# Two attention blocks in one kernel: layer 1's norm folded into weights, exponent and quotient, and the next sample's Q/K moved ahead of the projection

## The chip, the cores and the metric

The kernel runs on one core of one Trainium2 chip. The core has TensorE (matrix products, PE in the profile, with its weight loads shown apart as PEld), VectorE (DVE), ScalarE (ACT), GpSimd (POOL) and SyncE (SP), which issues nearly all DMAs. The metric is the device time of one execution in microseconds; lower is better. Before the change it is 2942.72 us, the median of three runs (2942.66 to 2943.72). The profiled execution took 2943.53 us, of which 2941.7 us lie between its first and its last instruction; all places in time below count from that first instruction.

## What is computed

For each of eight samples, an array of 512 channels by 1024 positions in f32, two attention layers run one after the other:

```python
def layer0(x):                      # 8 heads of 64 channels
    h = group_norm(x, 32 groups) * norm_w + norm_b
    q, k, v = split(qkv_w @ h + qkv_b)
    o = per head: softmax(q k^T / 8) v
    return x + proj_w @ o + proj_b

def layer1(x):                      # one head of 512 channels
    n = (x - mean) * rsqrt(var + eps)     # over the whole sample
    n = n * gn_gamma + gn_beta
    q, k, v = wq @ n + bq, wk @ n + bk, wv @ n + bv
    o = softmax(q k^T / sqrt(512)) v
    return x + wo @ o + bo
```

## The kernel before

**Joined weights.** Layer 1 never makes k, nor applies wo apart: before the loop `product` multiplies wq with wk and wv with wo into two weights, `wqk1` and `wvo1`. With them the scores are (wqk n)^T n, and the values are already projected. The biases go through the same products in `Through`: rows of bias copies times a weight, stored to DRAM, fetched back as columns and added up (`made["bias_q1"]`, `made["bias1"]`).

**Products in seven parts.** Every big product is a Strassen-Winograd step (`strassen`): seven half-size products of parts `A11` to `S4` of the one operand and `B11` to `T4` of the other. `finish` makes the `S` parts of a weight, `Combined` the `T` parts of the data. Partial results stay in one PSUM bank (`line`, copied by ScalarE to a tile `u`) and another (`single`). `strassen` is a generator that yields after each product; `together` takes two of them turn by turn, and `at_steps` hangs other work (hooks) on the numbers of these steps. TensorE, ScalarE and VectorE run in exactly the order in which the program was written (`manual_schedule`); SyncE's and GpSimd's orders are a scheduler's.

**One sample.** `layer0` makes v, then the second half of the heads' q and k (`pairs_qk(w, 1, ...)`), in whose steps the next sample's group norm is taken and its `T` parts are made. It then runs through 64 units (four pairs of heads in `ORDER`, two halves of the positions, eight blocks of keys): `scores` (L630), exp on ScalarE (L557), the running sum of the exponentials `acc` on VectorE (L559), and `values` two units later (L649). For a pair, `add_keys` (L663) multiplies `acc` with ones to add up over keys; `one_over` (L570) takes the reciprocal, `spread` (L579) copies it by DMA to the rows where it is wanted, `divide` (L669) applies it. The last pair, `end`, is treated half by half: the first half in the loop of units, the second in the first step of `project`, where VectorE's reciprocal stands ahead of the product's further parts (`combine1`, `combine2`, L713 and L719).

`project` (matmuls at L438) adds the result to x (L766) and takes the statistics of each finished piece at once (`of_half`, L297); `of_channels` (L300) ends them. After it the first half of the heads' q and k of the next sample is computed (`pairs_qk(..., 0, ...)`), and in its steps 4 to 9 the layer-1 norm is taken: the average of the means by a small matmul (`mean_of_all`, L278), the spread and its average (`variance_of_all`), the power -1/2 on GpSimd (L318), scale and shift applied to the data, x to `h` (`normed`, L336 and L338), and the `T` parts of `h`. For the last sample there is no next one, and these steps stand alone.

`attention1` then makes q from `h` (L438 again, bias added at L468 and L470), v (L453), the scores (L844), exp with a constant scale (L854), and the values (L901); at L929 and L930 the reciprocal and the bias are applied and x is added.

**Weights.** `next_weight` hands out a weight and asks for the one two places further on in the list `coming`; three buffers hold them. The first use of a weight loads four parts, finishes the `S` parts on VectorE and stores all seven to DRAM; later ones load the seven. Everything is issued on SP in one queue.

Of the kernel before, what the change touches and what calls it, by code (L numbers as in the profile page):

```python
# [58 lines left out]
def two_attention_blocks(  # L60
# [103 lines left out]
    extent = const.tile([P, B * 12], FP, tag="extent", name="extent")  # L164
# [16 lines left out]
    def finish(parts, a21):  # L181
        nc.vector.tensor_tensor(parts["S1"], a21, parts["A22"], ALU.add)
        nc.vector.tensor_tensor(parts["S2"], parts["S1"], parts["A11"], ALU.subtract)
        nc.vector.tensor_tensor(parts["S3"], parts["A11"], a21, ALU.subtract)
        nc.vector.tensor_tensor(parts["S4"], parts["A12"], parts["S2"], ALU.subtract)
# [4 lines left out]
    class Weight:  # L190
# [25 lines left out]
        def finish(self):  # L216
            for parts, rest in zip(self.parts, self.rest):
                finish(parts, rest)
            stored[self.name] = dram.tile([P, W_SIZE], FP, tag=self.name, name=f"stored_{self.name}")
            nc.sync.dma_start(stored[self.name], self.tile)  # L220
# [16 lines left out]
    for b in range(B):  # L237
        coming += ["qk13", "p0"] if b == 0 else ["v0", "qk13", "p0"]
        coming += ["qk02"] if b + 1 < B else []
        coming += ["wqk1", "wvo1"]  # L240
# [42 lines left out]
    class Norm:  # L283
# [3 lines left out]
        def __init__(self, xs, w, b, average, name):  # L287
            self.xs, self.w, self.b, self.average, self.name = xs, w, b, average, name
# [25 lines left out]
        def variance_of_all(self):  # L314
            var = self.average(self.spread, f"v_{self.name}")
            rstd = self.tile("rstd")
            nc.vector.tensor_scalar(rstd, var, EPS, None, ALU.add)
            nc.gpsimd.tensor_tensor(rstd, rstd, minus_half[:, : self.width], ALU.pow)  # L318
            scale = self.scale = self.tile("scale", NC)
            shift = self.shift = self.tile("shift", NC)  # L320
            w, b = vec[:, self.w : self.w + NC], vec[:, self.b : self.b + NC]
            if self.width == 1:
                nc.vector.tensor_scalar(scale, w, rstd, None, ALU.mult)
                nc.vector.tensor_scalar(shift, scale, self.mean, None, ALU.mult)
            else:
                nc.vector.tensor_tensor(scale, rstd, w, ALU.mult)
                nc.vector.tensor_tensor(shift, self.mean, scale, ALU.mult)
            nc.vector.tensor_tensor(shift, b, shift, ALU.subtract)

# [10 lines left out]
    def norm0(xs, b):  # L340
        return Norm(xs, V_NW0, V_NB0, group_average, f"0_{b}")

    def norm1(xs, b):
        return Norm(xs, V_NW1, V_NB1, sample_average, f"1_{b}")

    class Combined:
# [5 lines left out]
        def first(self, quarters):  # L352
            (b11, b12), (b21, b22) = quarters
# [3 lines left out]
            nc.vector.tensor_tensor(self.parts["T1"], b12, b11, ALU.subtract)  # L357
            nc.vector.tensor_tensor(self.parts["T2"], b22, self.parts["T1"], ALU.subtract)
            self.b12 = b12

        def second(self):
            p = self.parts
            nc.vector.tensor_tensor(p["T3"], p["B22"], self.b12, ALU.subtract)
            nc.vector.tensor_tensor(p["T4"], p["B21"], p["T2"], ALU.subtract)

    def combined(quarters, name):
        c = Combined(name)
        c.first(quarters)
        c.second()
        return c.parts  # L370
# [4 lines left out]
    def strassen(multiply, done, name):  # L375
# [11 lines left out]
        line = banks("s", f"ps_{name}_0")[:, 0, :]  # L387
        multiply(line, "A11", "B11", True)
        copied(1)
        single = banks("o", f"ps_{name}_1")  # L390
        single, spare[0] = single[:, 0, :], single[:, 1, :]
# [99 lines left out]
    def many(v_bias, name):  # L491

        t = tile2(f"many_{name}")[:, 0, :P].rearrange("p (c m) -> p c m", c=NC)
        at = vec[:, v_bias : v_bias + NC]
        nc.vector.tensor_copy(t, at.unsqueeze(2).to_broadcast([P, NC, P // NC]))
        return t

    class Through:
# [4 lines left out]
        def __init__(self, moving, many, bias, name, ps):  # L503
            self.bias, self.name, self.ps = bias, name, ps
            for cc in range(NC):
                for to, w in moving(cc):
                    rows = ps[cc * (P // NC) : (cc + 1) * (P // NC), to]
                    nc.tensor.matmul(rows, many[:, cc, :], w, start=True, stop=True)

        def store(self):  # L510
            row = tile2(f"row_{self.name}")[:, 0, :]
            nc.scalar.copy(row, self.ps)
            self.shares = dram.tile([NC, C], FP, tag=self.name, name=f"shares_{self.name}")
            for cc in range(NC):
                nc.sync.dma_start(self.shares[cc : cc + 1], row[cc * (P // NC) : cc * (P // NC) + 1, :])

        def fetch(self):
            self.columns = const.tile([P, NC, NC], FP, tag=f"c_{self.name}", name=f"c_{self.name}")
            for cc in range(NC):
                nc.sync.dma_start(  # L520
                    self.columns[:, cc, :], self.shares[cc].rearrange("(o p) -> p o", p=P)
                )

        def add(self):
# [927 lines left out]
```

## Time and profile before

| | |
|---|---|
| median of three runs | 2942.72 us |
| span of the profiled execution | 2941.7 us |
| mean granted TensorE clock | 0.997 |
| instructions | 33922 |
| reciprocal of 128x512 on VectorE, mean | 3355 ns |
| 128x512 elementwise on VectorE with two tensors, mean | 680 to 692 ns |
| the same with a column and two tensors, mean | 733 to 752 ns |
| 128x1024 combination on VectorE, mean | 1217 to 1225 ns |
| period of a sample, start of one `project` reciprocal wait to the next | 359.91 us |

In a line of a timeline the first number is the start, the second the length, then follow the engine, the line of the kernel, the operation, output and inputs with their shape, and the number of instructions merged into the row; in brackets stands how long the engine was idle before it, and on whom it had waited. An f32 matmul is recorded as two instructions. The ends of matmuls are modelled, so two rows may overlap by a tenth or two of a microsecond; starts are measured.

### The profile page before, as it was taken

The numbers are of one execution on the slowest core, as the hardware profiler recorded it, in microseconds if no ns is written. First come the engines' busy times: TensorE is split into PE (matmuls) and PEld (weight loads), VectorE is DVE, ScalarE is ACT, GpSimd is POOL, SyncE is SP. The second block draws the span as 40 slices with busy tenths as digits, with TensorE's granted clock in tenths as the row PEclk, the third lists the DMA queues.
The fourth block names the chain that finished last, engine by engine and source line by source line (L and its number), as shares of the span: only waits on it lengthen the run. The fifth ranks groups of instructions, "written<-read, shape, count | busy, mean of one in ns | idle before, by whom it ended". The sixth has DMA issues, their size and how long they took to land.

```text
span 2941.7 us, 33922 instructions
## 1 busy us (share of the span) xinstructions
PE 2912.1 (99%) x14018; PEld 1357.8 (46%) x14018; DVE 1753.0 (60%) x2142; ACT 1069.8 (36%) x1512; POOL 13.9 (0%) x26
## 2 busy tenths in 40 slices
PE   9999999999999999999999999999999999999898
PEld 4434554345533455335553354533545335453353
DVE  4586265853668536684357844578355773547825
ACT  2462214622156221552216522264222642226321
POOL 0000000000000000000000000000000000000000
PEclk9999999999999999999999999999999999999999
DMA  7301122011220103102031021210212112120001
GB/s 269 133 23 51 50 93 79 23 50 50 93 87 16 68 33 118 62 16 75 25 118 62 15 76 54 89 64 23 80 47 96 56 33 75 43 96 20 8 0 37
DMA packets 63403, 184.27 MB, mean 63 GB/s; under 512 B 13309, under 2 KB 13821, under 8 KB 56841
## 3 DMA queue, kind: packets, MB, share of 16 engines
q1 hardware_dynamic: 63096, 182.01, 18.1%
q8 instruction: 112, 1.84, 0.3%
q14 instruction: 51, 0.41, 0.0%
q10 hardware_dynamic: 144, 0.02, 0.0%
HBM read 137.41 MB, written 27.81 MB: 56 GB/s over the span
## 4 chain that ended last, share of the span: by engine, by line
PE 95%; DVE 4%; ACT 1%; issue 0%; DMA 0%; SPq 0%; POOL 0%; DVEq 0%; POOLq 0%
PE s L630 15%; PE ps_o L649 14%; PE ps_v L453 13%; PE ps_o L901 13%; PE ps_q L438 13%; PE ps_s L844 13%; PE ps_k L438 7%; PE ps_p L438 4%; DVE inv L570 1%; PE ps_sum L663 1%; DVE acc L559 1%; PE ps_wvo L540 1%; PE ps_wqk L540 0%; DVE t_p L713 0%; DVE t_p L719 0%; ACT p L557 0%
## 5 line engine op out<-in xcount | busy, mean ns | idle before, releaser
L557 ACT ACTIVATE p<-s 128x1024 f32<-128x1024 f32 x512 | 523.5, 1024 | 313.6 <-PE s L630 310.9
L630 PE MATMUL s<-q,k 64*64 64x512 f32 x4096 | 532.5, 591 | 0.0
L649 PE MATMUL ps_o<-p,v 64*64 64x512 f32 x4096 | 528.7, 589 | 0.0
L559 DVE TENSOR_TENSOR acc<-acc,p 128x1024 f32<-128x1024 f32 x384 | 468.4, 1220 | 80.2 <-ACT p L557 62.9
L630 PEld LDWEIGHTS s<-q,k 64*64 64x64 f32 x4096 | 151.9, 133 | 294.7 <-issue 254.4
L649 PEld LDWEIGHTS ps_o<-p,v 64*64 64x64 f32 x4096 | 156.6, 133 | 282.8 <-issue 280.3
L852 DVE TENSOR_TENSOR p<-ps_s,u_s 128x512 f32<-128x512 f32 x96 | 66.4, 691 | 249.8 <-ACT u_s L385 139.4
L487 DVE TENSOR_TENSOR v<-ps_v,u_v 128x512 f32<-128x512 f32 x96 | 66.1, 689 | 202.3 <-PE ps_v L453 130.6
L385 ACT COPY u_v<-ps_v 128x512 f32<-128x512 f32 x96 | 56.2, 585 | 326.4 <-PE ps_v L453 326.4
L385 ACT COPY u_q<-ps_q 128x512 f32<-128x512 f32 x96 | 56.2, 585 | 317.4 <-PE ps_q L438 317.3
L844 PE MATMUL ps_s<-s_q,t 128*128 128x512 f32 x384 | 167.4, 592 | 0.0
L901 PE MATMUL ps_o<-t_p,s_v 128*128 128x512 f32 x384 | 166.1, 592 | 0.0
L559 DVE TENSOR_TENSOR acc<-p,p 128x1024 f32<-128x1024 f32 x64 | 78.4, 1224 | 98.9 <-ACT p L557 98.9
L438 PE MATMUL ps_p<-t_p,w_p 128*128 128x512 f32 x256 | 113.3, 595 | 5.4 <-DVE inv L570 5.4
L470 DVE SCALAR_TENSOR_TENSOR q<-ps_q,bias_q,u_q 128x512 f32<-128x512 f32 x48 | 36.0, 750 | 137.0 <-ACT u_q L385 74.8
L844 PEld LDWEIGHTS ps_s<-s_q,t 128*128 128x128 f32 x384 | 73.0, 190 | 91.8 <-issue 91.8
L901 PEld LDWEIGHTS ps_o<-t_p,s_v 128*128 128x128 f32 x384 | 73.0, 190 | 91.8 <-issue 89.9
L901 PE MATMUL ps_o<-p,v 128*128 128x512 f32 x256 | 113.3, 595 | 0.0
L453 PE MATMUL ps_v<-w_wvo,t 128*128 128x256 f32 x512 | 113.1, 379 | 0.0
L438 PE MATMUL ps_q<-t,w_wqk 128*128 128x512 f32 x256 | 112.5, 592 | 0.0
L844 PE MATMUL ps_s<-q,h 128*128 128x512 f32 x256 | 112.5, 592 | 0.0
L570 DVE RECIPROCAL inv<-ps_sum 128x512 f32<-128x512 f32 x32 | 107.4, 3355 | 7.1 <-ACT held_sum L566 7.1
(208 smaller groups left out, 3593.2 us busy)
## 6 DMA issues: line engine op xcount, KB each, us to landing
x<-in_x SPq DMA_DIRECT2D x92, 512.0 KB
w_qk<-stored_qk SPq DMA_DIRECT2D x14, 1792.0 KB
out<-x SPq DMA_DIRECT2D x32, 512.0 KB
w_wqk<-stored_wqk SPq DMA_DIRECT2D x8, 1792.0 KB
w_wvo<-stored_wvo SPq DMA_DIRECT2D x8, 1792.0 KB
w_v<-stored_v SPq DMA_DIRECT2D x7, 1792.0 KB
w_p<-stored_p SPq DMA_DIRECT2D x7, 1792.0 KB
inv<-inv SPq DMA_DIRECT2D x192, 64.0 KB
```

What stands on the lines that cost most here:

```text
L385: nc.scalar.copy(us[n], line)
L438: nc.tensor.matmul(bank, w[a][:, k, c * P : (c + 1) * P], bs[b][:, k, :], start=fresh and k == 0, stop=k == 1, skip_group_check=True,)
L453: nc.tensor.matmul(bank[:, u * 2 * P : (u + 1) * 2 * P], bs[b][:, k, n * P : (n + 1) * P], w[a][:, k, :], start=fresh and u == k == 0, sto ...
L487: nc.vector.tensor_tensor(v, pairs(bank), pairs(u), ALU.add)
L557: nc.scalar.activation(p, s, AF.Exp, scale=factor)
L559: nc.vector.tensor_tensor(acc, first, p, ALU.add)
L570: nc.vector.reciprocal(inv, ps)
L630: nc.tensor.matmul(s[cols, j, :], flat(ks[pair])[rows, k0 : k0 + HD], qs[pair][rows, g, :], start=True, stop=True,)
L649: nc.tensor.matmul(o[cols, half, :], vs[kt][rows, c0 : c0 + HD], p[rows, j, :], start=kt == 0, stop=kt == NT - 1,)
L844: nc.tensor.matmul(bank, bs[b][:, k, t * P : (t + 1) * P], q_parts[a][:, k, :], start=fresh and k == 0, stop=k == 1, skip_group_check=True,)
L852: nc.vector.tensor_tensor(p, bank, u, ALU.add)
L901: nc.tensor.matmul(bank, v_parts[kt // 2][a][:, kt % 2, c * P : (c + 1) * P], p_parts[kt // 2][b][:, kt % 2, :], start=fresh and kt == 0, ...
```

## The change

- **Layer 1 no longer norms the data.** Gamma is multiplied into the rows of `wvo1` and `wqk1` (`scale_rows`) and into q as ScalarE's scale; the constant part of the norm goes through the weights as further bias rows (`Rows` and `Through` with two sets of rows, for beta and for gamma); 1/deviation squared becomes part of exp's scale (`norm.factor`), and 1/deviation a factor of the quotient (`norm.rstd`). q, v and the scores are made of raw x. Mean and deviation are needed for q's bias (`untaken`: `norm.c`) and for the last bias (`bias`).
- **The two averages, the `T` parts of x and the small operations after them move into the steps of q's own product** in `attention1`. `strassen` gets the argument `fine`, which adds a step after the first product.
- **The next sample's first Q/K goes ahead of the projection**, right after the units. The last pair is then summed over both halves at once in its step 3, its reciprocal spread by DMA like the others', the division done at step 8 and the rest of the projection's parts at step 9. Only the last sample keeps the old order (`last`). The list `coming` is reordered to suit.
- **Scaling and finishing of `wvo1` and `wqk1` move to GpSimd**; the rows for `wvo1` go into the product of `wqk1`, those for `wqk1` into step 3 of the first Q/K.

```diff
-        coming += ["qk13", "p0"] if b == 0 else ["v0", "qk13", "p0"]
+        coming += ["qk13"] if b == 0 else ["v0", "qk13"]
         coming += ["qk02"] if b + 1 < B else []
-        coming += ["wqk1", "wvo1"]
+        coming += ["p0", "wqk1", "wvo1"]
...
+        def scale_rows(self, engine, by):
+            for cc in range(NC):
+                for _, a in self.moving(cc):
+                    engine.tensor_scalar(a, a, vec[:, by + cc : by + cc + 1], None, ALU.mult)
...
+        def untaken(self):
+            rstd, mean = self.rstd, self.mean
+            over, self.c, self.factor = self.tile("over"), self.tile("c", NC), self.tile("factor")
+            nc.vector.reciprocal(over, rstd)
+            nc.vector.tensor_scalar(self.c, made["q_g"], mean, None, ALU.mult)
+            nc.vector.scalar_tensor_tensor(self.c, made["q_b"], over, self.c, ALU.mult, ALU.subtract)
+            nc.vector.tensor_scalar(self.factor, rstd, rstd, C**-0.5, ALU.mult, ALU.mult)
...
+        if not last:
+            name = f"0_{b}_{end}"
+            hooks = {
+                1: [combine1],
+                2: [lambda: combine2(2, 0), lambda: combine2(3, 0), lambda: combine2(4, 0)],
+                3: [lambda: sum_both(end, room(f"sum_{name}"), name)],
+                6: [lambda: held(invs.pop(end), f"inv_{name}")],
+                8: [lambda: divide_both(end)],
+                9: [lambda: combine2(2, 1), lambda: combine2(3, 1), lambda: combine2(4, 1)],
+            }
+            at_steps(
+                together(*pairs_qk(next_weight(), 0, combine.parts, qs_next, ks_next, b + 1)), hooks
+            )
...
-                first = i == half == 0
+                first = last and i == half == 0
...
-        at_steps(together(*[
-            make_channels(
-                w, c, c, bs, made["bias_q1"], lambda chunk, half: piece(qs, chunk, half), f"q_1_{b}"
-            )
-            for c in range(2)
-        ]), {})
+        combine, later = Combined(f"1_{b}"), []
+        combine.take(xs)
+        bs = combine.parts
...
+            return strassen(by_channels(w, c, bs), done, f"q_1_{b}_{c}", True)
+        at_steps(together(make_q(0), make_q(1)), {
+            0: [norm.mean_of_all, lambda: combine.make(1)],
+            1: [norm.deviation],
+            2: [norm.untaken],
+            3: [lambda: combine.make(2), lambda: later.pop(0)(), lambda: later.pop(0)()],
+            5: [lambda: combine.make(3)],
+            7: [lambda: combine.make(4)],
+        })
+        bias = norm.bias()
...
-                nc.scalar.activation(p, bank, AF.Exp, scale=C**-0.5)
+                nc.scalar.activation(p, bank, AF.Exp, scale=norm.factor)
...
-                    nc.vector.tensor_tensor(u, bank, invs[1][:, j, :], ALU.mult)
                     nc.vector.scalar_tensor_tensor(
-                        x, u, made["bias1"][:, chunk : chunk + 1], x, ALU.add, ALU.add
+                        u, bank, norm.rstd, invs[1][:, j, :], ALU.mult, ALU.mult
+                    )
+                    nc.vector.scalar_tensor_tensor(
+                        x, u, bias[:, chunk : chunk + 1], x, ALU.add, ALU.add
                     )
...
-        wvo1.finish()
         spare[0] = banks("o", "ps_norm")[:, 0, :]
-        manys = [many(V_BV1, "bias1"), many(V_BQ1, "bias_q1")]
-        taken = product(wqk1, nq1, nk1, "s", [norm.mean_of_all, norm.variance_of_all])
+        norm1_vectors = many(V_NB1, "norm1", V_NW1)
...
+                super().__init__(sets, 2, name, ps)
+                self.store()
+                w.scale_rows(nc.gpsimd, V_NW1)
...
+            wvo1.finish(nc.gpsimd)
...
+        taken = product(wqk1, nq1, nk1, "s", {
+            (0, 3): [through_v], (2, 1): [norm.mean_of_all], (2, 3): [norm.variance_of_all]
+        })
...
-            together(*pairs_qk(w, 0, bs, qs, ks, 0)), {2: [wqk1.finish], 8: [waiting[0].finish]}
+            together(*pairs_qk(w, 0, combine.parts, qs, ks, 0)), {3: [through_q], 8: [waiting[0].finish]}
```

## The prediction

> **What bounds the kernel now.** I read the busy totals and the chain of waits first, then TensorE's own timeline for its gaps, then the other engines inside each gap.
>
> ```profile
> PE 2912.1 (99%) x14018; PEld 1357.8 (46%) x14018; DVE 1753.0 (60%) x2142; ACT 1069.8 (36%) x1512; POOL 13.9 (0%) x26
> PE 95%; DVE 4%; ACT 1%; issue 0%; DMA 0%; SPq 0%; POOL 0%; DVEq 0%; POOLq 0%
> ```
>
> TensorE is busy for 2912.1 of 2941.7 us. The work taken off VectorE and ScalarE (the layer-1 norm's passes over the data) is beside it and worth nothing by itself. Only what TensorE executes, or the 30 us in which it waits, can move the time. A 512-column record of its starts 0.429 us after the one before (eight take 3.43 us). In a middle sample its timeline has one wait, in the projection:
>
> ```profile
> 594.63 3.70 PE L438 MATMUL ps_p<-o,w_p 128*128 128x512 f32 x8
> 598.82 1.55 PE L438 MATMUL ps_p<-t_p,w_p 128*128 128x512 f32 x3 [0.50 <-DVE inv L570]
> ```
>
> 594.63 + 3.43 = 598.06, so 0.76 us are lost to the reciprocal of the last head pair. The timeline of all engines at the end of that projection:
>
> ```profile
> 614.38 1.88 PE L438 MATMUL ps_p<-o,w_p 128*128 128x512 f32 x4
> ...
> 616.09 3.60 PE L438 MATMUL ps_q<-x,w_qk 128*128 128x512 f32 x8
> ...
> 617.42 0.67 DVE L780 TENSOR_TENSOR u_p<-ps_p,u_p 128x512 f32<-128x512 f32 x1
> ...
> 618.13 0.75 DVE L766 SCALAR_TENSOR_TENSOR x<-u_p,bias,x 128x512 f32<-128x512 f32 x1
> ...
> 618.91 0.69 DVE L297 BATCH_NORM_STATS2 part<-x 128x6 f32<-128x512 f32 x1
> ...
> 619.52 0.47 DVE L300 BATCH_NORM_AGGREGATE stat<-part 128x2 f32<-128x12 f32 x4
> ```
>
> TensorE is through with the projection at 616.09 and goes straight on with the next Q/K; VectorE has the statistics of x only at 619.99, 3.9 us later. Now nobody waits for them. In the last sample there is no next Q/K, and TensorE's timeline shows the wait in the open:
>
> ```profile
> 2774.44 1.88 PE L438 MATMUL ps_p<-o,w_p 128*128 128x512 f32 x4
> 2780.11 0.59 PE L278 MATMUL ps_m<-stat,in_sample 128*128 128x4 f32 x2 [3.79 <-DVE stat L300]
> 2781.62 0.59 PE L278 MATMUL ps_v<-spread,in_sample 128*128 128x4 f32 x2 [0.92 <-DVE spread L312]
> 2784.65 5.64 PE L438 MATMUL ps_q<-h,w_wqk 128*128 128x512 f32 x8 [2.44 <-DVE h L338]
> ```
>
> The eight records after it take 5.64 us in place of 3.60. The view by stretches says why (columns: stretch, length, busy PE, PEld, DVE, ACT, POOL, granted clock, DMA):
>
> ```profile
> 2396.07:2399.49 3.42, 1.86 (x6) 0.55 (x4) 3.39 (x3) 1.63 (x3) 0.00 (x0) 1.00 0.00 0
> 2399.49:2402.90 3.41, 3.41 (x8) 1.56 (x9) 3.41 (x6) 0.00 (x0) 0.00 (x0) 1.00 0.00 0
> 2774.95:2778.36 3.41, 1.37 (x4) 0.30 (x2) 3.31 (x6) 0.00 (x0) 0.00 (x0) 1.00 0.01 2
> 2778.36:2788.60 10.24, 5.13 (x9) 2.86 (x10) 7.41 (x21) 3.06 (x5) 0.55 (x1) 0.50 0.00 0
> ```
>
> After 1.37 us of work in 3.41 the clock is halved; after 1.86 it is not.
>
> **What the Trainium skill says.** "TensorE: Matmul & The Clock Gate", Part 1 (The HAM clock gate), gives a free-running window of 3.413 us, after an idle one of which the clock is halved until a busy one. The trace agrees on the grid (10.24 us is three windows), not on "idle": 1.37 us of work did not save the clock. "GPSIMD Engine Reference", section 3.1, gives 4497 ns for a two-input f32 operation of 2048 elements on GpSimd, so I estimate 1.12 us for 512; the trace has no such operation there.
>
> **The change part by part.**
>
> *Gains on TensorE.* (1) The last pair's sums are taken once over both halves: two groups of 128*64 records (8.6 us over 8 samples each, 1.08 per group) become one of 128*32 (25.6/192 x 8 = 1.07), in seven samples: -7.5 us. (2) With the next Q/K (24 us) ahead of the projection, the reciprocal and the copies of its result are hidden: a copy like it took from 2371.8 to 2380.2, 8.4 us; the sum can be taken 11.4 us into the stage, ScalarE's read and the reciprocal end near 15.7, the copies near 24, and the projection reads the divided half near 27. So the new wait on DMA costs nothing by 3 us. The division's ten VectorE operations (3.35 + 1.22 + 8 x 0.68 = 10.0 us) and ScalarE's two come into a stage in which VectorE was busy for 13.2 of 24.6 us, and the old norm's leave it. Weight requests move too: the projection's weights are asked for after those of this Q/K, still a stage (24 us) ahead, against 6 us for such a transfer (50.96 to 56.97). The gaps removed are 0.76 in five samples, 1.13 in the first, 1.83 in the seventh: -6.8 us. (3) The last sample's norm: the projection ends at 2776.16, and the first eight Q records end at 2790.29 where 3.43 us would do: -10.3 us, allowing for the two averages. Gains: 24.6 us.
>
> *The wait that appears.* In every sample layer 1's Q now follows the projection at once. TensorE's order is: first product of one half (four records, 1.72 us), the average of the means, first product of the other half, the average of the spreads. The first needs raw x, which is there; the average needs the statistics, which come 3.95 us after the projection's end, as VectorE's tail (6 pieces, all in the same order) is unchanged. Queued behind that small matmul is everything TensorE has. 3.95 - 1.72 = 2.23, with refilling 2.3 us, eight times: +18.4 us. The second average is hidden: its input took 1.14 us (628.11 to 629.25), the product ahead of it 1.72. POOL's power (0.55 us), the four small operations after it and the extra scalings on ScalarE fit ahead of what needs them by a microsecond or more. T1 to T4 of raw x (1.22 us each) come a product ahead of their use. Exp with a scale from memory, the quotient's extra factor (0.75 for 0.69 us) and the bias lie beside TensorE.
>
> *Before the loop.* Two sets of bias rows, each 4 products of 512 and 8 of 256 columns in 32-column groups, cost 2.1 us each (the rows of before: 8 records in 0.88, 16 half as wide in 1.02, transitions 0.2); 1.95 us of old rows go. The first set delays the norm's averages by 2.1, so the start of Q (38.27) too. The scaling of W_vo and its combinations go to POOL ahead of the power:
>
> ```profile
> 32.70 1.01 POOL L318 TENSOR_TENSOR rstd<-rstd,minus_half 128x4 f32<-128x4 f32 x1 [30.70 <-DVE rstd L317]
> ...
> 38.27 3.70 PE L438 MATMUL ps_q<-x,w_qk 128*128 128x512 f32 x8 [0.73 <-ACT rest_wqk L550]
> ...
> 50.96 0.45 SPq L220 DMA_DIRECT2D stored_wqk<-w_wqk  x1
> ...
> 58.31 2.27 SPq L119 DMA_DIRECT2D x<-in_x  x4
> ```
>
> POOL starts near 26.9; eight scalings near 0.4 us (guessed between memset's 0.20 and affine select's 0.34 for half the width, doubled) and four combinations of 1.12 make 7.7, to 34.6; the power could start at 34.8. Taken: 0.5 us late, bounds 0 and 6. Q starts +2.6, and the second set adds 2.1: +4.7. The same POOL work on W_qk holds SP's queue: its store moves from 51 to about 61.5, and behind it stand the weights of the second Q/K, another store, a reload and the next x. At the rates of the stretches 52 to 56 (a store, 455 GB/s) and 60 to 68 us (x, 345 GB/s) these 6.6 MB take 16 us and x is complete near 86, while V, starting near 67.4, needs VectorE past two of its four parts at 86.2. Taken: +1.5, bounds 0 and 8.
>
> *The clock.* A 2.1 us idle stretch that falls wholly within one window leaves 1.3 us of work, like the window that halved the clock. Between 1.37 and 1.86 the limit is unknown, so 0.4 to 0.65 of all phases trip it. A tripped window costs 1.6 us. The phases aren't random: the period, 359.91 us less 1.9 plus 2.3, is 105 windows and 1.9; from a miss the next sample lands in a hit, and a hit's own 1.6 us brings the period to 106 windows less a trifle, which repeats the hit. Lowest: nothing; highest: all eight, 13 us. Taken: six, +9.5, and +1.5 for the stalls before the loop.
>
> Sum: 18.4 + 4.7 + 1.5 + 11.0 - 24.6 = +11.0: 2952.7 us against this profile's span of 2941.7, or 2953.7 beside the other runs (2942.7, a microsecond above the span).
>
> **Rivals.** *The clock holds.* Without the 11.0 the sum is 0: 2943 us, no change. For it: the window before 2399.49 held with 1.86. Against it: the new stretch is longer than that one. It decides if a window with 1.3 us of work doesn't trip. *Faster: the statistics come early.* Were VectorE not behind at the projection's end, its last piece needs 0.68 + 0.75 + 0.69 + 0.47, about 2.5 us; the wait is then 0.8, the clock holds, and 2931 us follow. It decides from a lead of 1.4 us. Against it: VectorE is busy without a break over the last six pieces, and none of that work is removed. *POOL is slow before the loop.* At twice the estimate Q starts 8 us later and x comes late by as much again: about 2968. For it: nothing in the trace bounds those operations from above. That Q/K ahead waits for the copies of the reciprocal is within the range.
>
> **How the numbers follow.** My forecast 0.52 (2946 to 2961), clock holds 0.22 (2939 to 2948), statistics early 0.11, slow POOL 0.15. Two in ten are left out by 2941 to 2966. A measurement tells 0.2%, 5.9 us, from no change: slower gets nearly all of the first and the fourth, 0.63; same 0.25; faster 0.12.
>
> **What would show it.** Right: in each sample an idle of about 2.1 us ahead of the average of the means, released by the statistics, and half clock after most; no gap on the reciprocal but in the last sample; Q of sample 0 near 41. Wrong: an idle under 1 us there, or a clock that stays whole.

## The result

The changed kernel takes 2969.34 us (median of four runs, 2968.41 to 2972.41), the kernel before 2943.09 (four runs, 2942.66 to 2943.72): a ratio of 1.0091, 95% interval 1.0073 to 1.0108. It is slower, as forecast, but by 26.2 us where 11.0 were forecast, and 3 us above the range. The profiled execution has a span of 2967.1 us at a mean granted clock of 0.993 (before: 2941.7 at 0.997).

TensorE's own timeline splits the difference. The first run of sixteen score products of layer 0 (`s<-q,k ... x16`) marks the end of all that is done once. In the kernel before, the products of V (`ps_v`) start at 62.41, the second Q/K follows at 86.58 and the score run at 115.90; in the changed kernel the score run starts at 138.42:

```profile
62.41 7.07 PE L453 MATMUL ps_v<-w_v,x 128*128 128x256 f32 x32
...
86.58 3.60 PE L438 MATMUL ps_q<-x,w_qk 128*128 128x512 f32 x8
...
115.90 1.95 PE L630 MATMUL s<-q,k 64*64 64x512 f32 x16
```

```profile
138.42 1.95 PE L681 MATMUL s<-q,k 64*64 64x512 f32 x16
```

| | start of the score run | from there to the end |
|---|---|---|
| before | 115.90 | 2825.8 |
| changed | 138.42 | 2828.7 |
| difference | +22.5 | +2.9 |
| by the prediction's terms | +7.7 | +3.3 |

The second column of the last row is 18.4 + 9.5 - 24.6, the first 4.7 + 1.5 + 1.5. So the loop as a whole did what was forecast, and nearly all that is missing lies ahead of it.

**The loop.** The busy totals and the chain of waits of the changed kernel:

```profile
PE 2917.9 (98%) x14050; PEld 1363.1 (46%) x14050; DVE 1720.0 (58%) x2135; ACT 1088.3 (37%) x1500; POOL 38.7 (1%) x52
PE 93%; DVE 4%; POOL 1%; DMA 1%; SPq 0%; ACT 0%; issue 0%; DVEq 0%; POOLq 0%; ACTq 0%
```

VectorE's 33 us less busy time bought nothing, as said. POOL's share of the chain, 0% before, is 1%. TensorE's timeline of a middle sample, from the projection on:

```profile
998.71 7.03 PE L477 MATMUL ps_p<-o,w_p 128*128 128x512 f32 x16
1005.57 12.18 PE L477 MATMUL ps_p<-t_p,w_p 128*128 128x512 f32 x28
...
1022.74 1.88 PE L477 MATMUL ps_q<-x,w_wqk 128*128 128x512 f32 x4
1026.70 0.53 PE L296 MATMUL ps_q<-stat,in_sample 128*128 128x4 f32 x2 [2.08 <-DVE stat L318]
```

The gap that stood between the first two rows of the projection (0.50 before) is gone; in its place TensorE waits after layer 1's first product: that product would be through at 1022.74 + 1.72 = 1024.46, and the average of the means starts at 1026.70, 2.24 us later. (In the last sample it is 2.32.) The waits of TensorE that differ from those before, from the view of waits (us in total, times, longest):

```profile
PE ps_q L296 <- DVE stat L318: 16.7, 8, 2.2
PE ps_v L492 <- DVE v L526: 8.2, 1, 8.2
PE ps_q L477 <- ACT rest_wqk L602: 6.7, 1, 6.7
...
PE ps_p L477 <- DVE inv L622: 1.2, 1, 1.2
```

The first line is the wait in all eight samples, the last the reciprocal, left in the last sample alone. The second and third stand before the loop. The clock after the wait, by stretches (columns as above: stretch, length, busy PE, PEld, DVE, ACT, POOL, granted clock, DMA):

```profile
299.75:303.16 3.41, 2.55 (x6) 0.77 (x5) 3.32 (x5) 0.59 (x1) 0.00 (x0) 1.00 0.47 118
303.16:306.57 3.41, 2.18 (x8) 1.23 (x9) 2.79 (x11) 0.00 (x0) 0.00 (x0) 1.00 0.96 412
661.57:664.98 3.41, 1.33 (x6) 0.48 (x4) 3.00 (x8) 0.59 (x1) 0.00 (x0) 1.00 0.89 294
664.98:668.39 3.41, 3.41 (x5) 1.43 (x6) 1.85 (x5) 0.00 (x0) 0.00 (x0) 0.50 0.57 244
```

In the first sample the wait lies across the edge of two windows, both keep over 2 us of work, and the clock holds. In the second it lies within one, 1.33 us are left, and the next window runs at half clock. That happens in five of the eight samples. (In the four other kernels below with the same loop it is five to seven, as the first sample falls at another place of the clock's grid in each.) A period (one average of means of layer 1 to the next) is 360.31 us without such a window and 362.0 with one: 1.69 us each.

**Before the loop.** POOL's timeline:

```profile
26.24 0.94 POOL L232 TENSOR_SCALAR w_wvo<-w_wvo,vec 128x256 f32<-128x256 f32 x1 [23.95 <-PE ps_rows L554]
...
33.45 1.27 POOL L190 TENSOR_TENSOR w_wvo<-w_wvo,rest_wvo 128x512 f32<-128x512 f32 x1
...
38.58 1.04 POOL L336 TENSOR_TENSOR rstd<-rstd,minus_half 128x4 f32<-128x4 f32 x1
57.80 0.93 POOL L232 TENSOR_SCALAR w_wqk<-w_wqk,vec 128x256 f32<-128x256 f32 x1 [18.17 <-PE ps_k L554]
...
68.93 1.27 POOL L191 TENSOR_TENSOR w_wqk<-w_wqk 128x512 f32<-128x512 f32 x1
```

Eight scalings take 7.2 us (26.24 to 33.45), four combinations 5.1 (to 38.58), together 12.3 us for each weight. VectorE had been idle for 12.08 us when it read the means at 32.05, so that the first six scalings had nothing of VectorE's beside them: 0.93 us is POOL's own time. The power of the first norm, whose input was ready at 34.74, runs behind them at 38.58. W_qk's last combination ends at 70.20. What that does to VectorE, to SP's queue, to the next sample's x and to TensorE, from their timelines:

```profile
39.66 0.16 DVE L343 TENSOR_TENSOR scale<-rstd,vec 128x4 f32<-128x4 f32 x1 [4.91 <-POOL rstd L336]
...
93.92 0.69 DVE L315 BATCH_NORM_STATS2 part<-x 128x6 f32<-128x512 f32 x1 [13.75 <-DMA x<-in_x]
96.72 1.88 DVE L315 BATCH_NORM_STATS2 part<-x 128x6 f32<-128x512 f32 x3 [2.11 <-DMA x<-in_x]
```

```profile
70.22 0.32 SPq L238 DMA_DIRECT2D stored_wqk<-w_wqk  x1
...
83.74 3.27 SPq L125 DMA_DIRECT2D x<-in_x  x4
```

```profile
44.18 2.08 PE L477 MATMUL ps_q<-x,w_qk 128*128 128x512 f32 x2 [6.70 <-ACT rest_wqk L602]
...
99.24 3.78 PE L492 MATMUL ps_v<-w_v,x 128*128 128x256 f32 x8 [8.21 <-DVE v L526]
...
107.45 1.02 PE L477 MATMUL ps_q<-x,w_qk 128*128 128x512 f32 x2
```

The store of W_qk is issued at 70.22 (before: 50.96), x at 83.74 (58.31). The statistics of x stand in VectorE's queue ahead of the evacuations of V; VectorE waits 13.75 and 2.11 us for x, TensorE 8.21 us for VectorE, and three windows (94.95 to 105.19) run at half clock.

By stages of TensorE's timeline, changed against before: start of Q 44.18 against 38.27, +5.9; the first Q/K (to the start of V) 27.7 against 24.1, +3.6; V 35.6 against 24.2, +11.4; the second Q/K to the score run 31.0 against 29.3, +1.7. The unrounded sum is +22.5. The last of the four is one half-clock window after the wait on the vectors of layer 0's bias rows; the kernel before has this wait too, but at another place in its window.

### The profile page after: what moved, and what is told of

Same layout as the page of the kernel before. It is cut to its first block, busy times and chain, and to the rows that moved or that the text cites. A ratio compares the mean times of both kernels' runs of the same rounds, so it can differ in the third digit from the quotient of the medians.

```text
span 2967.1 us, 34095 instructions
## 1 busy us (share of the span) xinstructions
PE 2917.9 (98%) x14050; PEld 1363.1 (46%) x14050; DVE 1720.0 (58%) x2135; ACT 1088.3 (37%) x1500; POOL 38.7 (1%) x52
## 4 chain that ended last, share of the span: by engine, by line
PE 93%; DVE 4%; POOL 1%; DMA 1%; SPq 0%; ACT 0%; issue 0%; DVEq 0%; POOLq 0%; ACTq 0%
PE s L681 15%; PE ps_o L700 14%; PE ps_o L1000 13%; PE ps_s L943 13%; PE ps_q L477 13%; PE ps_v L492 13%; PE ps_k L477 6%; PE ps_p L477 4%; DVE part L315 1%; DVE x L837 1%; PE ps_sum L714 1%; DVE u_p L851 1%; PE ps_wvo L592 1%; DMA x<-in_x 0%; DVE inv L622 0%
## 5 line engine op out<-in xcount | busy, mean ns | idle before, releaser
L953 ACT ACTIVATE p<-p,factor 128x512 f32<-128x512 f32 x96 | 69.3, 722 | 133.6 <-DVE p L951 133.6
L315 DVE BATCH_NORM_STATS2 part<-x 128x6 f32<-128x512 f32 x128 | 85.5, 688 | 50.1 <-DMA x<-in_x 47.7
L943 PE MATMUL ps_s<-q,x 128*128 128x512 f32 x256 | 112.5, 592 | 0.0
```

Of the source, the lines that this page charges most:

```text
L315: nc.vector.bn_stats(self.part[:, cc, half, :], piece(self.xs, cc, half))
L943: nc.tensor.matmul(bank, bs[b][:, k, t * P : (t + 1) * P], q_parts[a][:, k, :], start=fresh and k == 0, stop=k == 1, skip_group_check=True,)
L953: nc.scalar.activation(p, bank, AF.Exp, scale=norm.factor)
```

## The experiments

In each the comparison is with the changed kernel's 2969.3 us; the kernel before took 2942.6 to 2943.1 beside them. Two theories were to be told apart for the stretch before the loop: that POOL's length holds first the power and then, through SP's queue, x; or that the added rows on TensorE, or the order of SP's queue and its amount of data, do it. For the loop, the theory was that the wait and the half clock after it are the whole cost, and that the gains are real. Five of the kernels (the changed one, the first experiment and three that touch the loop alone) have the same work before the loop, and their score runs start between 136.39 and 138.42, as windows fall differently; so a difference of up to 2 us in that start tells nothing.

### POOL's work written behind the power

```diff
-                w.scale_rows(nc.gpsimd, V_NW1)
+        def finish_v():
+            wvo1.scale_rows(nc.gpsimd, V_NW1)
+            wvo1.finish(nc.gpsimd)
...
-            (0, 3): [through_v], (2, 1): [norm.mean_of_all], (2, 3): [norm.variance_of_all]
+            (0, 3): [through_v], (2, 1): [norm.mean_of_all], (2, 3): [norm.variance_of_all, finish_v]
```

> The scaling and the combinations of W_vo are issued on POOL behind the power of the first norm instead of ahead of it; nothing else changes. Theory (POOL's work on W_vo, 12.4 us in the changed kernel and 7.7 in the prediction, holds the power, and the power holds the first norm): the power runs at about 34.9, Q starts near 40.4 instead of 44.18, W_qk's work on POOL and what hangs on it move forward by the same 3.8, the score run starts near 134.6 instead of 138.42, and the time is about 2965.5 against 2969.3. Rival (the two sets of bias rows on TensorE, or VectorE's share of the norm, hold Q): Q stays later than 43, and the time is within 1 us of 2969.3.

2970.8 us, ratio to before 1.0094 (1.0077 to 1.0111): no change. POOL's timeline of this kernel says why that tells nothing about the theory:

```profile
36.15 1.26 POOL L191 TENSOR_TENSOR w_wvo<-w_wvo 128x512 f32<-128x512 f32 x1
37.37 1.04 POOL L336 TENSOR_TENSOR rstd<-rstd,minus_half 128x4 f32<-128x4 f32 x1
```

The power still ran last. The order written in the program binds TensorE, ScalarE and VectorE; POOL's is a scheduler's, and it left the order as it was. The edit did not do what it says, and neither theory is touched.

### W_qk's scaling and combinations on VectorE

```diff
-                w.scale_rows(nc.gpsimd, V_NW1)
+                w.scale_rows(nc.vector if w is wqk1 else nc.gpsimd, V_NW1)
...
-            wqk1.finish(nc.gpsimd)
+            wqk1.finish()
```

> W_qk's eight scalings and four combinations run on VectorE instead of POOL; W_vo's stay where the changed kernel has them. Theory (POOL holds W_qk's store until 70.2, and behind it on SP's queue stands x of the second sample, whose lateness stops VectorE and then TensorE in V at 99): the store is issued near 64 instead of 70.22, x some 6 us sooner than 83.74, the 8.2 us wait at 99.24 shrinks to about 2 and the three windows at half clock there to one or none; the score run starts near 128 instead of 138.42; time about 2959. Q still starts at 44.2. Rival (x's lateness is in the order of SP's queue and the amount of data, not in POOL): the wait at V stays above 6 us and the time above 2966. Second rival (VectorE's added 5 to 6 us delay its evacuations of Q and K): a new wait of more than 2 us on VectorE between 58 and 72.

2958.66 us, ratio 1.0053 (1.0036 to 1.0070): 10.7 us less. SP's and TensorE's timelines:

```profile
63.24 0.33 SPq L238 DMA_DIRECT2D stored_wqk<-w_wqk  x1
...
74.40 4.02 SPq L125 DMA_DIRECT2D x<-in_x  x4
```

```profile
44.38 5.51 PE L477 MATMUL ps_q<-x,w_qk 128*128 128x512 f32 x8 [6.68 <-ACT rest_wqk L602]
...
92.53 2.00 PE L492 MATMUL ps_v<-w_v,x 128*128 128x256 f32 x8 [0.96 <-DVE v L526]
```

The store goes out 7.0 us sooner, x 9.3 us sooner, the wait in V falls from 8.21 to 0.96, and V takes 25.4 us (72.41 to 97.81) in place of 35.6. The score run starts at 127.13, 11.3 us sooner. That the lateness of x was POOL's is shown: the amount of data is unchanged (188.7 MB), and so is the order of the store, the weights and x in SP's queue; only some fetches of single columns change places. Q, for which W_vo's work on POOL still stands ahead of the power, starts as late as in the changed kernel. VectorE's eight scalings take 0.35 us each (POOL: 0.93), and TensorE waits nowhere for them.

### Both edits together

> Both of the two edits together: W_vo's work on POOL behind the power, W_qk's on VectorE. Theory (the whole miss of some 15 us before the loop is POOL's length at two places): Q starts near 40.4, x is requested near 70, no wait of more than 2 us in V, the score run starts near 122 to 124 instead of 138.42, time about 2953 to 2955. Rival (the two places do not add up: with Q sooner, V is sooner too and meets the same late x): the score run starts later than 128 and the time is above 2959.

2958.16 us, ratio 1.0052 (1.0036 to 1.0069), the score run at 126.02. Since the first edit moves nothing, this is the run before it again, 0.5 us apart; it shows only how well two such runs agree. The 126.02 is 1.1 sooner than the run before it, within those 2 us.

### Both weights on VectorE

```diff
-                w.scale_rows(nc.gpsimd, V_NW1)
+                w.scale_rows(nc.vector, V_NW1)
...
-            wvo1.finish(nc.gpsimd)
+            wvo1.finish()
-            wqk1.finish(nc.gpsimd)
+            wqk1.finish()
```

> The scalings and combinations of both weights run on VectorE. The last pair of runs showed that writing POOL's work behind the power did not move it there: the power still ran last on POOL. Here it has POOL to itself. Theory (the power waits for W_vo's 12.4 us on POOL, 3.8 us longer than its input needs): the power runs within 1 us of its input, Q starts 3.8 us sooner than in the run with W_qk alone on VectorE (44.38), near 40.5, and the half clock in the first Q (5.51 us for eight records) is gone or shorter; the score run starts near 122 (127.13 there), time about 2953.5 (2958.7 there). Rival (VectorE's 5.2 us for W_vo come ahead of the first norm's reading of its means and hold the norm, or ScalarE's copies of W_qk hold Q): Q starts later than 43 and the time stays above 2957.

2953.47 us, ratio 1.0039 (1.0025 to 1.0053): 15.9 us less than the changed kernel. POOL's, VectorE's and TensorE's timelines:

```profile
33.59 1.01 POOL L336 TENSOR_TENSOR rstd<-rstd,minus_half 128x4 f32<-128x4 f32 x1 [31.29 <-DVE rstd L335]
```

```profile
29.58 0.68 DVE L191 TENSOR_TENSOR w_wvo<-w_wvo 128x512 f32<-128x512 f32 x1
31.12 0.16 DVE L290 COPY mean_m<-ps_norm 128x4 f32<-128x4 f32 x1 [0.86 <-PE ps_norm L286]
...
34.63 0.16 DVE L343 TENSOR_TENSOR scale<-rstd,vec 128x4 f32<-128x4 f32 x1 [1.20 <-POOL rstd L336]
```

```profile
39.16 5.26 PE L477 MATMUL ps_q<-x,w_qk 128*128 128x512 f32 x8 [2.59 <-ACT rest_wqk L602]
...
86.66 1.99 PE L492 MATMUL ps_v<-w_v,x 128*128 128x256 f32 x8 [0.56 <-DVE v L526]
```

VectorE does W_vo in a gap of its own and is idle again 0.86 us ahead of the means; the power runs at once; its reader waits 1.20 us where it waited 4.91, and Q starts at 39.16. The score run starts at 121.26, 17.2 us sooner than in the changed kernel and 5.4 later than before: +0.9 at Q, +3.6 in the first Q/K, +0.8 in V. What remains is thus less than the 7.7 of the prediction, and the first eight records of Q still take 5.26 us: the half clock there was not POOL's, or not only. In the kernel before the old bias rows stood ahead of Q, from 35.62 to 37.54, and TensorE waited 0.73 us; now the rows are elsewhere, TensorE waits 2.59, the window from 35.50 to 38.91 keeps 1.06 us of work, and the next runs at half clock. Of the +3.6 in the first Q/K, 1.9 are the second set of rows and 1.6 this window.

### The averages two products later

```diff
-            0: [norm.mean_of_all, lambda: combine.make(1)],
-            1: [norm.deviation],
-            2: [norm.untaken],
-            3: [lambda: combine.make(2), lambda: later.pop(0)(), lambda: later.pop(0)()],
-            5: [lambda: combine.make(3)],
+            0: [lambda: combine.make(1)],
+            2: [norm.mean_of_all],
+            3: [norm.deviation],
+            4: [lambda: combine.make(2), norm.untaken],
+            5: [lambda: later.pop(0)(), lambda: later.pop(0)(), lambda: combine.make(3)],
```

> In layer 1's Q the average of the means stands after three products in place of one, that of the spreads after four in place of two; T1 is made first on VectorE. Nothing is left out. Theory (the 2.24 us wait in each of eight samples is the average placed 2.23 us before its statistics; five windows at half clock follow from it at 1.69 each): both vanish, 8 x 2.24 + 5 x 1.69 = 26.4 us less, about 2943. Rival (the wait moves: T1, the deviation or the factor of c then come late for a product): a wait of 1 us or more is seen at another product of the same stage, and the time is above 2952. If only the waits vanish and the clock is still halved in some samples: about 2951.

2958.0 us, ratio 1.0052 (1.0036 to 1.0069): 11.3 less, not 26.4. TensorE's timeline of a middle sample:

```profile
664.76 0.28 PE L296 MATMUL ps_q<-stat,in_sample 128*128 128x4 f32 x2
...
665.84 1.98 PE L477 MATMUL ps_q<-x,w_wqk 128*128 128x512 f32 x4 [0.80 <-DVE mean_m L298]
...
668.68 0.39 PE L296 MATMUL ps_q<-spread,in_sample 128*128 128x4 f32 x2 [0.85 <-DVE u_q L891]
```

The statistics are no longer waited for, but two other waits took their place (the expectation's rival, in another form). The average of the means lies in the PSUM tile into which the next product goes, which waits until VectorE has read the average; and that of the spreads goes into a tile whose other half VectorE is still reading. Counted from start to start the two cost 2.0 us in every sample, hardly less than the 2.24. The period is 360.05 us in every sample, 0.26 less than the changed kernel's without a half-clock window (360.31). So nearly all the gain is the clock: the same idle time in two pieces trips no window. From the score run on this kernel is 11.2 us shorter (2817.5 against 2828.7), where 8 x 0.26 + 5 x 1.69 = 10.5 are accounted for.

### The averages in the unused half of the first product's tile

```diff
+        if beside:
+            return beside[0]
         return banks("s", f"ps_{name}")[:, 0, :] if spare[0] is None else spare[0]
...
-        line = banks("s", f"ps_{name}_0")[:, 0, :]
+        line = banks("s", f"ps_{name}_0")
+        if fine and not beside:
+            beside.append(line[:, 1, :])
+        line = line[:, 0, :]
...
+            0: [lambda: combine.make(1)],
+            2: [norm.mean_of_all],
+            3: [lambda: combine.make(2)],
+            4: [norm.deviation],
+            5: [lambda: combine.make(3), norm.untaken, lambda: later.pop(0)(), lambda: later.pop(0)()],
```

> Against the run with later averages, where 0.85 + 0.80 us of wait per sample were left because the averages share a PSUM tile with the products beside them, both averages go into the unused half of the first product's tile; the means after three products, the spreads after five. Theory (what was left there were waits on VectorE's reads of the shared tile): no wait above 0.3 us in layer 1's Q in any sample, no half clock after it, 8 x 2.24 + 5 x 1.69 = 26.4 us less than 2969.3, about 2943. Rival (the later c and factor then hold the evacuations of Q, and through them TensorE): a new wait of 1 us or more later in the stage, time above 2952.

2940.92 us, ratio 0.9994 (0.9985 to 1.0002): 28.4 less than the changed kernel, with its start before the loop as late as there (score run at 138.25). In the same place of a middle sample TensorE's timeline has no bracket any more:

```profile
663.37 0.28 PE L300 MATMUL ps_q<-stat,in_sample 128*128 128x4 f32 x2
663.51 1.96 PE L484 MATMUL ps_q<-x,w_wqk 128*128 128x512 f32 x4
```

The period is 357.96 us throughout, 2.35 less than 360.31. From the score run on it is 27.1 us shorter than the changed kernel, against 26.4 by the wait and the windows. The wait and its half clock are the whole cost of the new order, and nothing else comes up behind them.

### Filling the wait

```diff
+        def fill():
+            for _ in range(4):
+                nc.tensor.matmul(spare[0], ones, bs["B11"][:, 0, :], start=True, stop=True)
...
-            0: [norm.mean_of_all, lambda: combine.make(1)],
+            0: [fill, norm.mean_of_all, lambda: combine.make(1)],
```

> Four 128x512 products whose results nobody reads are added in every sample between layer 1's first product and the average of the means, where TensorE waits 2.1 us; all that is computed otherwise stays. Theory of the clock (five samples of eight run one window of 3.41 us at half clock because of that wait, 1.69 us each): the added work takes the place of the wait, no window in these stages is at half clock, and the time falls by about 8.4 us to 2961, though TensorE does 32 x 0.43 = 13.7 us more work. Rival (the half clock comes of something else, such as a power limit): the windows stay and the time is 2969 or more.

2967.37 us, ratio 1.0084 (1.0068 to 1.0101): 2.0 less, not 8.4. The expectation had one error in arithmetic: each f32 product is two records, so four of them are eight records and 3.43 us, not 1.72. TensorE's timeline, and a stretch of nearly one window's length from where the wait had been:

```profile
661.50 3.60 PE L909 MATMUL ps_q<-x,ones 128*128 128x512 f32 x8
...
664.94 0.28 PE L296 MATMUL ps_q<-stat,in_sample 128*128 128x4 f32 x2
```

```profile
662.20:665.60 3.40, 3.40 (x11) 1.56 (x10) 1.76 (x8) 0.09 (x1) 0.00 (x0) 1.00 0.99 426
```

The period is 361.4 us in every sample, never 1.69 more: no half clock. The filling is 1.19 us longer than the wait, 9.5 us in eight samples; the five windows saved are 8.4. From the score run on it takes 2828.9 us against 2828.7: the 2.0 us less are not of the loop but of the start, where the score run came at 136.39 in place of 138.42 and no window behind the bias vectors was at half clock. So the theory of the clock stands, with the price as counted: useless work in place of a wait cost no more than the wait did.

### Q/K back behind the projection

```diff
-        last = norm_next is None
+        last = True
...
+        if norm_next is not None:
+            at_steps(
+                together(*pairs_qk(next_weight(), 0, combine.parts, qs_next, ks_next, b + 1)), {}
+            )
```

The old call ahead of the projection, with its hooks, goes, and the weights are asked for in the old order.

> The next sample's Q/K stand behind the projection again, and the last head pair's sums, reciprocal and division are taken inside the projection in every sample, as in the kernel before; layer 1's norm stays untaken, with its weights scaled as in the changed kernel. Theory (the two halves of the change add): against 2969.3 the wait of 2.24 goes in seven samples (15.7) and the five half-clock windows with it (8.4), while the sums taken once (7.5) and the hidden reciprocal (6.8) are lost: about 2959.5. Rival (the gains on TensorE that the prediction counted were not real): about 2945. Rival (Q/K ahead costs nothing and gains much): 2969 or more.

2957.32 us, ratio 1.0048 (1.0032 to 1.0065): 12.0 less, 9.8 expected. The view of waits:

```profile
PE ps_p L478 <- DVE inv L623: 5.9, 8, 1.5
...
PE ps_q L297 <- DVE stat L319: 2.2, 1, 2.2
```

The wait on the statistics is left in the last sample, that on the reciprocal is back in all. The usual period is 359.91 us, that of the kernel before to the hundredth, and 1.95 longer than with Q/K ahead and no wait (357.96). That is terms (1) and (2) of the prediction, which had 1.07 + 0.76 = 1.83 for such a sample. So Q/K ahead is a gain, once its averages don't wait. The norm left untaken is worth something in the last sample alone: from the score run on 2820.6 us against 2825.8 before, with a wait of 2.2 us and a half-clock window still in it.

### What follows: both remedies

> The two remedies together: both weights scaled and combined on VectorE, both averages of layer 1 in the unused half of the first product's tile, the means after three products, the spreads after five. Theory (the stretch before the loop and the loop are independent): the score run starts near 121.3, as with both weights on VectorE, and the rest takes 2801.6 as in the run with the other half (2939.8 less 138.25): a span of 2923, a time near 2924, 0.6% under the kernel before. Rival (with the start moved, other windows of the clock are tripped, or transfers collide): 2930 or more.

Both weights on VectorE, both averages in the other half: 2925.41 us, ratio 0.9939 (0.9926 to 0.9953). 17.5 us faster than the kernel before, 43.9 faster than the changed one. The score run starts at 123.59, 2.3 us later than expected, as the window after the wait on the bias vectors (117.55 to 120.96) is at half clock here; the rest takes 2800.8.

The last run adds one edit: the vectors of layer 0's bias rows are copied ahead of the second Q/K instead of in it.

```diff
+            bias0_vectors = many(V_BV0, "bias0")
...
-                rows = Rows([(many(V_BV0, "bias0"), p0.moving)], 1, "bias0", room("bias0"))
+                rows = Rows([(bias0_vectors, p0.moving)], 1, "bias0", room("bias0"))
```

> As the run before it, and the vectors of layer 0's bias rows are copied on VectorE ahead of the second Q/K in place of in it, so that the 2.43 us wait of TensorE on that copy, which every kernel here has, goes. Theory: another 2.4 us less, near 2921.5. Rival (the wait is not the copy's but that of the evacuations of Q and K queued with it): no change from the run before it within 1 us.

2922.98 us, ratio 0.9933 (0.9920 to 0.9947), 2.4 less than the run before it. The times of the two overlap (2922.80 to 2926.14, and 2921.50 to 2923.22), so that it is the trace that shows the effect. The wait on the vectors is gone (in TensorE's timeline the rows start without a bracket), and the score run starts at 118.44:

```profile
110.96 1.88 PE L484 MATMUL ps_q<-x,w_qk 128*128 128x512 f32 x4
112.77 0.66 PE L561 MATMUL ps_k<-w_p,many_bias 128*32 128x256 f32 x8
```

These last 2.4 us have nothing to do with the change: the kernel before has the same wait.

## Why the prediction was wrong

**The step that failed** is in "Before the loop": "eight scalings near 0.4 us (guessed between memset's 0.20 and affine select's 0.34 for half the width, doubled) and four combinations of 1.12 make 7.7, to 34.6; the power could start at 34.8. Taken: 0.5 us late". The mechanism was right and named with its place; the size was not. A scaling takes 0.93 us, a combination 1.27, a weight 12.3 us. The combinations lie 13% above the estimate from "GPSIMD Engine Reference", section 3.1, in the Trainium skill; the scalings, for which neither the trace nor that section had a price, are 2.3 times the guess and carry most of the error. The guess was taken from a memset and an affine select, neither of which multiplies by a column; doubled, they give 0.40 to 0.68, of which the sum took the lower end, and even the upper end lies below the 0.93.

**What hung on it.** The power came 3.8 us late in place of 0.5, and Q at 44.18 in place of 40.9. W_qk's store went out at 70.22, not 61.5, and with it "x is complete near 86", "Taken: +1.5, bounds 0 and 8" became +11.4 in V: 8.2 us of wait and three half-clock windows, beyond even the upper bound. The path behind the store was right: 24.5 us were forecast from the store's issue to the end of x (61.5 to 86), and VectorE's last wait on x ends 26.5 us after it (70.22 to 96.72). The clock's term for this stretch, +1.5, stood for one window; six ran at half clock, some of them while TensorE waited anyway. With POOL's work taken away the stretch costs +5.4 in place of +22.5, so 17.2 of the 22.5 us are POOL's, 5.9 by way of the power (127.13 against 121.26) and 11.3 by way of W_qk's store (138.42 against 127.13). A part of these is half clock, not wait, and each is known to some 2 us.

This was the rival "POOL is slow before the loop", given 0.15, with 2968 at twice the estimate; the measured length is 1.6 times it. The bound above was open ("nothing in the trace bounds those operations from above"), and the range of 2966 cut it off all the same.

**The new wait** was right: 2.23 us forecast, 2.24 measured, in eight samples, released by the statistics; filled or taken away it is worth what was counted.

**The clock** was right in kind and nearly in number: six windows at 1.6 us forecast, five at 1.69 found. That it was so near is in part luck, as the same loop gave five to seven in other kernels. The rival "the clock holds" falls: a window with 1.33 us of work tripped. Two sums are off: by the prediction's own figures the share of phases that trip runs from 0.4 to 0.7, not 0.65, and a period with a hit, 358.4 + 1.9 + 1.6 = 361.9 us, is 106 windows (361.8) and a trifle, not less a trifle; 362.0 was measured, so each hit lies some 0.2 us later in its window than the last, until one misses. That a hit repeats itself also showed: the run with both weights on VectorE has such a window in each of the first six samples (periods of 361.95 to 362.0 us), the changed kernel in four of these six and in the seventh.

**The gains** were right: 1.95 us per middle sample against 1.83, and no wait of the projection on the reciprocal, weights or copies but on the reciprocal in the last sample. Term (3), forecast at 10.3, came to 9.2: from its score run on, the last sample takes 305.50 us before and 296.31 with the averages in the other half. The loop as a whole, 2.9 against 3.3, is the sum of these and the costs.

The rival **"the statistics come early"** needed them 1.4 us sooner; it falls by the wait of 2.24 us, which no sample undercuts.

## What to carry to other kernels

When work goes to an engine on which the trace shows nothing like it, price it from both sides and follow what stands behind it on that engine and in every queue that waits for its result; here 4.6 us too few for each of two weights came back as some 15. A short wait of TensorE cost more than its length when it fell within one window of the clock (1.69 us on top of 2.24), so move it or split it; to fill it with 3.43 us of useless work gained nothing here; and before moving a small product, look at which PSUM tile it writes and who reads that tile next. A change that is slower as it stands may hold a gain: here Q/K ahead of the projection was worth 1.95 us a sample as soon as the average no longer waited.

## What the runs showed of the hardware

A one-input scaling by a column on POOL (128x256, f32) takes 0.93 us, 3.6 ns for an element of a row, while a two-input combination of twice the width takes 1.27, 2.5 ns; VectorE does the two in 0.35 and 0.69.

The limit below which a window halves the clock lies a little over 1.4 us of work in 3.41, narrower than the 1.37 to 1.86 of the prediction. In the view by stretches of the changed kernel:

```profile
1385.19:1388.60 3.41, 1.42 (x4) 0.35 (x2) 3.31 (x9) 0.59 (x1) 0.00 (x0) 1.00 0.81 252
1388.60:1392.01 3.41, 3.32 (x11) 1.89 (x12) 2.19 (x8) 0.59 (x1) 0.47 (x1) 1.00 0.67 286
...
1747.01:1750.42 3.41, 1.43 (x5) 0.90 (x6) 2.76 (x12) 0.53 (x1) 0.00 (x0) 1.00 0.89 374
1750.42:1753.83 3.41, 3.41 (x7) 1.49 (x6) 1.27 (x3) 0.59 (x1) 0.56 (x1) 0.50 0.23 99
```

The window with 1.42 us did not trip, that with 1.43 did; the ends of products are modelled, so the two figures can't be told apart, but the edge is near. The other runs agree: of the windows at full clock in all their traces none with 1.41 us or less was followed by full clock, and none with 1.44 or more by half clock. In the Trainium skill "TensorE: Matmul & The Clock Gate", Part 1 (The HAM clock gate), speaks of an idle window; here one that is 40% busy counts as idle.

Some of VectorE's operations are longer beside POOL's work: the last step of the spread took 0.41 us, the addition of epsilon 0.56 and one combination of W_v 1.43 in the changed kernel, 0.16, 0.17 and 0.68 where POOL had no such work beside them. "SBUF — State Buffer", section "SBUF: two separate sides", says in the Trainium skill that VectorE, in an operation with two inputs or in a two-port mode, and GpSimd lock a port pair against each other for whole instructions. That agrees with these three in part only: the two steps of the spread just ahead, also of two inputs, took their 0.16 us beside POOL's scalings. No run here tells the lock from another cause.
